# Four graph layers on 32 groups: TensorE transposes replaced by VectorE block transposes and a trip through DRAM, with layers 0 and 1 run further ahead

## Chip, cores and metric

The kernel runs on one core of a Trainium2 chip. The metric is the device time in microseconds (us) of one execution. Five engines work side by side, each through its own queue of instructions: TensorE (PE, matmuls; PEld in the profile is its loading of the stationary operand), VectorE (DVE), ScalarE (ACT), GpSimd (POOL) and SyncE (SP, which here only issues DMAs). An instruction may wait for semaphores; everything behind it in the same queue waits with it.

## What is computed

There are 128 graphs of 128 nodes with 256 features, and an integer adjacency per graph. Four layers follow each other, and each is followed by a residual sum and a LayerNorm:

```python
x = _layernorm(x + L0(x, adj, a0, a1, a2, a3))  # 4 edge scores e_k = leaky(x*a_k @ x^T), where(adj==k+1, e_k),
                                                # softmax over j, alpha @ x
x = _layernorm(x + L1(x, adj, W_msg, W_upd, bias))  # relu(x @ W_upd + mean over neighbours of x @ W_msg + bias)
x = _layernorm(x + L2(x, adj, weight, w_ih, ...))   # 3 rounds of a GRU cell:
#     m = h @ weight[i]; aggr = A^T @ m
#     r = sigmoid(i_r + h_r); z = sigmoid(i_z + h_z); n = tanh(i_n + r * h_n); h = (1 - z) * n + z * h
x = _layernorm(x + L3(x, adj, W, a))  # Wh = x @ W; e = leaky(f_i + f_j); softmax(where(adj > 0, e, -1e9)); elu(alpha @ Wh)
```

All is in 32-bit floats, and the output has the shape of x.

## The kernel before

Four graphs make a group (G = 4, T = 4 x 128 = 512 columns), so there are 32 groups (NG). A matrix of one group stands either "tokens first" (128 nodes on the partitions, graph and feature along the row) or "features first" (128 of the 256 features on the partitions, KC = 2 such halves, and 512 graph-and-node columns). A PE matmul contracts over the partitions, so the kernel turns matrices from one form into the other again and again. It does so on PE: a transpose is a matmul against the identity `ident`, which writes a PSUM bank, from which ACT or DVE copies it to SBUF.

- `head(g)` holds layers 0 and 1 of group g. It loads x and adj, turns x (`features_first`, L236/L237), does four rounds of scaled scores (POOL and ACT make `xs`, PE L308, a predicated copy L309), a softmax, turns the probabilities (`columns_first`, L261/L263), multiplies by x (L328), normalises, turns x1 (L236), then layer 1: the product with W_upd and W_msg (L349), the product with the adjacency (L358), LayerNorm, and turns x2 into hT (L236).
- `gru(s)` holds layer 2. Each of its NL = 3 rounds has, for each half c, an aggregate over neighbours (`aggregate`, L406, copied to `agT` by ACT L410) and gates: `terms` (L418) adds products with the hidden state hT (`w_hhT`) and with the aggregate (`c_gi`) in one PSUM bank. `hidden` (L426), `reset` (L431, L432), `candidate` (L436 add, L438 tanh, L440 subtraction on POOL) and `update` (L446 tanh, L447, L449) make the new state. The aggregate needs the state tokens first: `tokens_first` (L390) turns it, `h_tokens` (L395) copies it to SBUF.
- `tail(g)` holds layer 3: it turns the GRU's result (L390, added at L509), statistics, the product with w3 (L519), a broadcast by transpose (L529), the masked softmax, the turn of the probabilities (L261), the product (L556), ELU (L560 to L570), LayerNorm and the output DMA (L575).

`run` writes the order of emission: `gru(g)` is the main line, `tail(g-1)` and `head(g+1)` are side lines. Every `yield took, gap, pe` gives an estimate of the PE time just emitted and the time after which the line may go on; a counter `clock` adds these. The Tile framework's scheduler may still move instructions on an engine, since it orders them by its own model. All PSUM tiles come from one pool of eight banks (`bank()`), and each wait is a semaphore that the framework sets.

DMAs are issued by SP alone: two loads and one output per group. DMAs go round eight completion lanes, and a DMA first waits for the one before it on its lane.

Of the kernel before, what the change touches and what calls it, by code (L numbers as in the profile page):

```python
# [17 lines left out]
def kernel(  # L18
# [29 lines left out]

    nc = tc.nc
# [15 lines left out]
    psum = ctx.enter_context(tc.tile_pool(name="psum", bufs=8, space=bass.MemoryType.PSUM))  # L65

    def bank():
        return psum.tile([P, 512], F32, tag="ps", name="ps")
# [6 lines left out]
    def load(g):  # L75
        xg = inputs.tile([P, G, D], F32, tag="x_in", name="x_in")
        nc.sync.dma_start(out=xg, in_=x[g * G : (g + 1) * G].rearrange("b n d -> n b d"))
        ag = inputs.tile([P, G, N], I32, tag="adj_in", name="adj_in")
        nc.sync.dma_start(out=ag, in_=adj[g * G : (g + 1) * G].rearrange("b i j -> i b j"))
        return xg, ag  # L80

    loaded = {0: load(0)}


# [22 lines left out]

    def weights():

        nats = []  # L110
        for src in (w_ih, w_hh):
            nat = work.tile([P, NGC, D], F32, tag="hu", name="nat")
            nc.sync.dma_start(out=nat, in_=src.rearrange("(g p) d -> p g d", p=P))
            nats.append(nat)
            if src is w_ih:
                wnat = []
                for i in range(NL):
                    w = work.tile([P, KC, D], F32, tag="q", name="wnat", bufs=3)
                    nc.sync.dma_start(out=w, in_=weight[i].rearrange("(c p) e -> p c e", p=P))
                    wnat.append(w)  # L120
# [10 lines left out]
        w_ihT = [work.tile([P, 3 * D], F32, tag="wh", name="w_ihT") for c in range(KC)]  # L131
        for nat, dst in zip(nats, (w_ihT, [w_hhT[:, c] for c in range(KC)])):
            for c in range(KC):
                for g0, g1 in ((0, 4), (4, NGC)):
                    ps = bank()
                    for g in range(g0, g1):
                        nc.tensor.transpose(
                            ps[:, (g - g0) * P : (g - g0 + 1) * P], nat[:, g, c * P : (c + 1) * P], ident
                        )
                    nc.any.tensor_copy(dst[c][:, g0 * P : g1 * P], ps[:, : (g1 - g0) * P])  # L140
                    yield 0.4, 0.0


        for i in range(NL):
# [7 lines left out]
            nc.any.tensor_copy(wT, ps.rearrange("p (e d) -> p e d", e=KC))  # L152
            yield 0.4, 1.0
            for d in range(KC):
                for n0, n1 in ((0, 512), (512, 3 * D)):
# [9 lines left out]
                    nc.any.tensor_copy(c_gi[:, i, d, n0:n1], ps[:, : n1 - n0])  # L165
# [24 lines left out]

    def statistics(res, out):
# [3 lines left out]
        for b in range(G):  # L197
# [3 lines left out]
            if b == 1:  # L201
                yield 0.0, 1.5, False
        nc.vector.tensor_scalar_add(rstd, mv[:, :, 1], EPS)  # L203
        nc.gpsimd.tensor_tensor(rstd, rstd, neg_half, OP.pow)  # L204
        out.extend((mv, rstd))

    def normalise(res, mv, rstd, tag, bufs, out):
        nmr = work.tile([P, G], F32, tag="nmr", name="nmr", bufs=4)
        nc.vector.scalar_tensor_tensor(nmr, mv[:, :, 0], -1.0, rstd, op0=OP.mult, op1=OP.mult)  # L209
        xn = work.tile([P, G, D], F32, tag=tag, name=tag, bufs=bufs)  # L210
        for b in range(0, G, 2):
            nc.vector.tensor_scalar(
                xn[:, b, :], res[:, b, :], mv[:, b, 0:1], rstd[:, b : b + 1],
                op0=OP.subtract, op1=OP.mult,
            )
        yield 0.0, 0.5, False
        for b in range(1, G, 2):
            nc.scalar.activation(  # L218
                xn[:, b, :], res[:, b, :], AF.Identity, bias=nmr[:, b : b + 1], scale=rstd[:, b : b + 1]
            )  # L220
        out.append(xn)

    def layernorm(res, tag, bufs, out):
        got = []
        yield from statistics(res, got)
        yield 0.0, 2.5, False
        yield from normalise(res, *got, tag, bufs, out)

    def features_first(xn, tag, bufs):

        xT = []
        for c in range(KC):
            t = work.tile([P, T], F32, tag=tag, name=tag, bufs=bufs)
            ps = bank()
            for b in range(G):
                nc.tensor.transpose(ps[:, b * N : (b + 1) * N], xn[:, b, c * P : (c + 1) * P], ident)  # L236
            nc.scalar.copy(t, ps)  # L237
            xT.append(t)
        return xT

    def softmax(alpha, out):
# [4 lines left out]
        p = work.tile([P, G, N], F32, tag="prob", name="prob", bufs=3)  # L246
# [6 lines left out]
        yield 0.0, 3.0, False  # L253
        rinv = work.tile([P, G], F32, tag="rinv", name="rinv", bufs=4)
        nc.vector.reciprocal(rinv, rs)
        out.extend((p, rinv))

    def columns_first(p):
        ps = bank()
        for b in range(G):  # L260
            nc.tensor.transpose(ps[:, b * N : (b + 1) * N], p[:, b, :], ident)  # L261
        pT = work.tile([P, G, N], F32, tag="probT", name="probT")
        nc.scalar.copy(pT, ps.rearrange("p (b n) -> p b n", b=G))  # L263
        return pT
# [6 lines left out]

    def head(g, s):
        xg, ag = loaded.pop(g)
# [4 lines left out]
        a_f = work.tile([P, G, N], F32, tag="a_f", name="a_f")  # L282
        nc.gpsimd.tensor_copy(a_f, ag)
        alpha = work.tile([P, G, N], F32, tag="alpha", name="alpha")
        nc.gpsimd.memset(alpha, NEG0 / SLOPE)
        mk = work.tile([P, 4, G, N], U8, tag="mk", name="mk")
        s.m_gt = work.tile([P, G, N], U8, tag="m_gt", name="m_gt", bufs=3)
        s.a_ne = work.tile([P, G, N], F32, tag="a_ne", name="a_ne")


        xT = features_first(xg, "xT", 4)
        yield 0.9, 1.0, False
        for k in range(4):
            nc.vector.tensor_scalar(mk[:, k], a_f, float(k + 1), None, op0=OP.is_equal)
            yield 0.0, 1.0
            ps = bank()
            xs = []
            for c in range(KC):
# [5 lines left out]
                xs.append(t)  # L304
            for b in range(G):
# [3 lines left out]
            nc.vector.copy_predicated(alpha.rearrange(FLAT), mk[:, k].rearrange(FLAT), ps)  # L309
            yield 1.8, 0.5, False  # L310
        yield 0.0, 0.5, False

        leaky(alpha, alpha, 0.0)
        nc.vector.tensor_scalar(s.m_gt, a_f, 0.0, None, op0=OP.is_gt)
        yield 0.0, 1.5, False
        got = []
        yield from softmax(alpha, got)
        p, rinv = got
        nc.vector.tensor_scalar(s.a_ne, a_f, 0.0, None, op0=OP.not_equal)
        yield 0.0, 0.0  # L320
        pT = columns_first(p)
        yield 0.45, 1.5
        res = work.tile([P, G, D], F32, tag="res", name="res", bufs=3)
# [11 lines left out]
        yield 1.75, 2.0, False  # L335
        got = []
        yield from layernorm(res, "xa", 1, got)
        x1 = got[0]
        yield 0.0, 2.0


        xT = features_first(x1, "xT", 4)
        yield 0.9, 2.0
        hu = work.tile([P, G, 2 * D + 1], F32, tag="hu", name="hu")
        nc.gpsimd.memset(hu[:, :, 2 * D : 2 * D + 1], 1.0)
        for b in range(G):
            ps = bank()
            for c in range(KC):
                nc.tensor.matmul(  # L349
                    ps, xT[c][:, b * N : (b + 1) * N], w_um[:, c, :], start=(c == 0), stop=(c == KC - 1)  # L350
                )
# [3 lines left out]
        res = work.tile([P, G, D], F32, tag="res", name="res", bufs=3)  # L355
        for b in range(G):
# [14 lines left out]
            if b % 2:  # L371
                yield 0.9, 2.5, b == 1
        got = []
        yield from layernorm(res, "xb", 3, got)
        s.x2 = got[0]
        yield 0.0, 2.0
        s.hT = features_first(s.x2, "hT", 8)
        yield 0.9, 1.5

    def gru(s):
        hT = s.h0T = s.hT
        hn = [s.x2[:, :, c * P : (c + 1) * P] for c in range(KC)]

        def tokens_first(c, h):

# [268 lines left out]
```

## Time and profile before

| what | us |
|---|---|
| time, median of 3 runs (lowest to highest) | 3246.43 (3245.19 to 3246.86) |
| the profiled execution, its time | 3246.94 |
| span of the profiled execution on the core | 3245.2 |
| mean granted PE clock | 0.992 |
| first GRU matmul (L418) starts | 77.7 |
| GRU matmuls of one group, PE passes of 512 columns | 144 |
| last GRU matmul starts; last output DMA issued | 3210.6; 3241.4 |

A line of groups in the profile reads: line, engine, operation, tile written<-tiles read, shape, xcount | busy us, mean ns of one | idle time of the engine before them and what ended it. "Busy" of PE overlaps: matmuls are pipelined, so the time that one adds to PE's path is read from starts in the timeline, not from its mean. In this trace one 32-bit matmul stands as two PE instructions, and a transpose as one. A chain line tells which work the last instruction can be followed back through. "PEld issue" is time in which nothing that the profile shows is waited for. A line of DMA issues ends with the median us from issue to landing.

The groups of the GRU's elementwise work lie at 0.68 to 0.72 us for 128x512 on ACT and DVE, and at 1.3 us on POOL (L440). Every sixth to eighth group is 1.6 us longer than the others.

### The profile page before, as it was taken

The numbers are of one execution on the slowest core, as the hardware profiler recorded it, in microseconds if no ns is written. First come the engines' busy times: TensorE is split into PE (matmuls) and PEld (weight loads), VectorE is DVE, ScalarE is ACT, GpSimd is POOL, SyncE is SP. The second block draws the span as 40 slices with busy tenths as digits, with TensorE's granted clock in tenths as the row PEclk, the third lists the DMA queues.
The fourth block names the chain that finished last, engine by engine and source line by source line (L and its number), as shares of the span: only waits on it lengthen the run. The fifth ranks groups of instructions, "written<-read, shape, count | busy, mean of one in ns | idle before, by whom it ended". The sixth has DMA issues, their size and how long they took to land.

```text
span 3245.2 us, 32948 instructions
## 1 busy us (share of the span) xinstructions
PE 3137.9 (97%) x11992; PEld 1836.3 (57%) x11992; DVE 1563.0 (48%) x4022; ACT 1362.6 (42%) x2768; POOL 802.4 (25%) x679
## 2 busy tenths in 40 slices
PE   7999999999999999999999999999999999999997
PEld 4556555556555565555565555555555655555654
DVE  3445455544455454545444554545454445544443
ACT  3344434444344444344444444444444444444443
POOL 2122222222221222222222212222212222122221
PEclk8999999999999999999999999999999999999998
DMA  2000000000000000000000000000000000000000
GB/s 80 10 14 10 11 17 17 17 13 11 10 17 17 14 11 10 17 17 17 14 10 11 17 17 14 10 11 17 17 17 14 11 10 17 13 14 1 7 7 13
DMA packets 56995, 47.60 MB, mean 15 GB/s; under 512 B 4353, under 2 KB 56705, under 8 KB 56833
## 3 DMA queue, kind: packets, MB, share of 16 engines
q1 hardware_dynamic: 56832, 45.50, 4.4%
q8 instruction: 95, 1.56, 0.2%
q14 instruction: 68, 0.55, 0.1%
HBM read 28.72 MB, written 16.78 MB: 14 GB/s over the span
## 4 chain that ended last, share of the span: by engine, by line
PE 79%; DVE 10%; POOL 5%; ACT 4%; issue 1%; DMA 0%; ACTq 0%; POOLq 0%; SPq 0%; DVEq 0%
PE ps L418 49%; PE ps L349 7%; PE ps L308 7%; PE ps L406 4%; PE ps L519 3%; PE ps L390 3%; DVE st L199 3%; POOL rstd L204 2%; DVE res L570 2%; POOL res L566 2%; PE ps L236 2%; PE ps L358 2%; DVE res L331 2%; ACT res L563 1%; ACT xa L218 1%
## 5 line engine op out<-in xcount | busy, mean ns | idle before, releaser
L418 PE MATMUL ps<-hT,w_hhT 128*128 128x512 f32 x2304 | 1088.8, 593 | 0.0
L418 PE MATMUL ps<-agT,c_gi 128*128 128x512 f32 x2304 | 1061.6, 592 | 0.0
L418 PEld LDWEIGHTS ps<-agT,c_gi 128*128 128x128 f32 x2304 | 430.1, 190 | 466.9 <-issue 453.5
L418 PEld LDWEIGHTS ps<-hT,w_hhT 128*128 128x128 f32 x2304 | 406.3, 191 | 342.5 <-issue 319.0
L440 POOL TENSOR_TENSOR t_d<-hT,t_n 128x512 f32<-128x512 f32 x192 | 248.8, 1296 | 984.4 <-ACT t_n L438 596.1
L447 DVE SCALAR_TENSOR_TENSOR t_d<-t_z,t_d 128x512 f32<-128x512 f32 x192 | 132.3, 689 | 433.3 <-ACT t_z L446 377.8
L349 PE MATMUL ps<-w_um,xT 128*128 128x512 f32 x512 | 251.6, 616 | 63.4 <-ACT xT L237 63.4
L308 PEld LDWEIGHTS ps<-xs,xT 128*128 128x128 f32 x2048 | 249.9, 193 | 60.7 <-issue 53.8
L432 DVE SCALAR_TENSOR_TENSOR t_r<-t_r,q 128x512 f32<-128x512 f32 x192 | 134.5, 700 | 306.0 <-ACT t_r L431 306.0
L204 POOL TENSOR_TENSOR rstd<-rstd,neg_half 128x4 f32<-128x4 f32 x128 | 143.0, 1117 | 559.7 <-DVE rstd L203 559.7
L308 PE MATMUL ps<-xs,xT 128*128 128x128 f32 x2048 | 250.4, 276 | 0.0
L426 ACT ACTIVATE q<-ps,bhn 128x512 f32<-128x512 f32 x192 | 131.9, 687 | 278.0 <-PE ps L418 278.0
L301 POOL TENSOR_SCALAR xs<-xT,acol 128x512 f32<-128x512 f32 x128 | 201.0, 1576 | 136.3 <-PE ps L308 123.5
L446 ACT ACTIVATE t_z<-ps,brz 128x512 f32<-128x512 f32 x192 | 131.9, 687 | 203.8 <-PE ps L418 203.8
L199 DVE BATCH_NORM_STATS2 st<-res 128x6 f32<-128x256 f32 x512 | 200.7, 408 | 1.1
L349 PEld LDWEIGHTS ps<-w_um,xT 128*128 128x128 f32 x512 | 94.8, 195 | 184.5 <-ACT xT L237 95.9
L431 ACT ACTIVATE t_r<-ps,brz 128x512 f32<-128x512 f32 x192 | 130.4, 679 | 159.0 <-PE ps L418 159.0
L410 ACT COPY agT<-ps 128x512 f32<-128x512 f32 x192 | 112.8, 588 | 181.3 <-PE ps L406 173.5
L218 ACT ACTIVATE xb<-res,nmr,rstd 128x256 f32<-128x256 f32 x128 | 73.4, 598 | 271.8 <-DVE nmr L209 271.8
L309 DVE COPY_PREDICATED alpha<-mk,ps 128x512 f32<-128x512 uint8 x128 | 93.1, 728 | 193.2 <-PE ps L308 193.1
L438 ACT ACTIVATE t_n<-t_r,bih 128x512 f32<-128x512 f32 x192 | 138.7, 723 | 110.4 <-DVE t_r L436 110.4
L406 PEld LDWEIGHTS ps<-a_ne,hn 128*128 128x128 f32 x1024 | 134.2, 191 | 34.5 <-issue 31.1
(97 smaller groups left out, 3506.3 us busy)
## 6 DMA issues: line engine op xcount, KB each, us to landing
x_in<-in_x_dram SPq DMA_DIRECT2D x32, 512.0 KB, 3.4
out_dram<-xb SPq DMA_DIRECT2D x32, 512.0 KB, 2.9
adj_in<-in_adj_dram SPq DMA_DIRECT2D x32, 256.0 KB, 2.7
nat<-in_L_gnn_w_ih_dram SPq DMA_DIRECT2D x1, 768.0 KB, 5.1
wnat<-in_L_gnn_weight_dram SPq DMA_DIRECT2D x3, 256.0 KB, 5.5
nat<-in_L_gnn_w_hh_dram SPq DMA_DIRECT2D x1, 768.0 KB, 7.3
w_um<-in_L_gnn_W_upd_dram SPq DMA_DIRECT2D x1, 256.0 KB, 7.6
w_um<-in_L_gnn_W_msg_dram SPq DMA_DIRECT2D x1, 256.0 KB, 7.4
```

What stands on the lines that cost most here:

```text
L199: nc.vector.bn_stats(st, res[:, b, :])
L204: nc.gpsimd.tensor_tensor(rstd, rstd, neg_half, OP.pow)
L301: nc.gpsimd.tensor_scalar(t, xT[c], acol[:, k, c : c + 1], None, op0=OP.mult)
L308: nc.tensor.matmul(ps[:, cols], xT[c][:, cols], xs[c][:, cols], start=(c == 0), stop=(c == KC - 1))
L349: nc.tensor.matmul(ps, xT[c][:, b * N : (b + 1) * N], w_um[:, c, :], start=(c == 0), stop=(c == KC - 1))
L406: nc.tensor.matmul(ps[:, b * N : (b + 1) * N], hn[c][:, b, :], s.a_ne[:, b, :], start=True, stop=True)
L418: nc.tensor.matmul(gates[q], w[:, q * P : (q + 1) * P], v, start=(start and n == 0), stop=(stop and n == len(ops) - 1),)
L426: nc.scalar.activation(t, ps, AF.Identity, bias=bhn[:, c : c + 1], scale=0.5)
L432: nc.vector.scalar_tensor_tensor(t, t, 1.0, q, op0=OP.add, op1=OP.mult)
L438: nc.scalar.activation(n, t, AF.Tanh, bias=bih[:, 2 * KC + c : 2 * KC + c + 1], scale=1.0)
L440: nc.gpsimd.tensor_sub(d, hT[c], n)
L447: nc.vector.scalar_tensor_tensor(d, z, 1.0, d, op0=OP.add, op1=OP.mult)
```

## The change

The change does five things.

1. Transposes no longer go through PE and PSUM, except for the weights and the broadcast in layer 3. The new `turned` lets DVE transpose blocks of 32x32 inside a [128, 512] matrix, writes the result to a DRAM tile with four DMAs, one for each 32 partitions, in runs of 32 floats (128 bytes), and reads it back with one DMA in rows of 512 floats, so that the blocks stand where the full transpose has them. It is used for layer 0's and layer 3's probabilities, for x1 (two halves), for hT (two), and for the new state of each half in each round (six): 12 times a group.
2. x is loaded a second time as blocks: eight DMAs of 32x16x32 floats per group, and two DVE transposes make the features-first form (the old load of rows stays, for the product and the residual).
3. `head` is split into `layer0` and `layer1`; while `gru(g)` runs, the side lines are layer 3 of g-1, layer 1 of g+1 and layer 0 of g+2. Layers 0 and 1 of group 0 and layer 0 of group 1 run ahead of the first GRU.
4. The scheduler no longer reorders: `manual_schedule` keeps each engine in the order of emission. `run` now emits a piece of the GRU's matmuls, up to two side steps without PE, the GRU's elementwise step, then one side step with PE. The GRU's order within a round is new: all products with the hidden state come first, then both aggregates, then the rest.
5. PSUM has two tags of four banks each: "gate" for the r and z gates, "ps" for all else. LayerNorms normalise in place; two steps of layer 3 and the softmax exponentials are emitted in halves.

```diff
-    psum = ctx.enter_context(tc.tile_pool(name="psum", bufs=8, space=bass.MemoryType.PSUM))
+    psum = ctx.enter_context(tc.tile_pool(name="psum", bufs=4, space=bass.MemoryType.PSUM))
+    dram = ctx.enter_context(tc.tile_pool(name="dram", bufs=4, space=bass.MemoryType.DRAM))
+    ctx.enter_context(tc.manual_schedule())
+    def bank(tag="ps"):
+        return psum.tile([P, 512], F32, tag=tag, name=tag)
...
     def load(g):
+        xb = inputs.tile([P, KC, 4 * G, 32], F32, tag="x_blocks", name="x_blocks", bufs=1)
+        for c in range(KC):
+            for j in range(4):
+                f0 = c * P + j * 32
+                nc.sync.dma_start(
+                    out=xb[j * 32 : (j + 1) * 32, c],
+                    in_=x[g * G : (g + 1) * G, :, f0 : f0 + 32].rearrange("b (i r) f -> r (b i) f", r=32),
+                )
...
+    def turned(dst, src):
+        n = src.shape[1]
+        z = work.tile([P, 4, n, 32], F32, tag="z", name="z", bufs=3)
+        nc.vector.transpose(z.rearrange("p j n f -> p n j f"), src.rearrange("p n (j f) -> p n j f", f=32))
+        way = dram.tile([32, 4, n, 4, 32], F32, tag="way", name="way")
+        for i in range(4):
+            nc.sync.dma_start(
+                out=way[:, :, :, i, :].rearrange("f j n t -> f (j n) t"),
+                in_=z[i * 32 : (i + 1) * 32].rearrange("f j n t -> f (j n) t"),
+            )
+        nc.sync.dma_start(
+            out=dst, in_=way.rearrange("f j n i t -> j f (n i t)")
+        )
...
     def softmax(alpha, out):
...
-        out.extend((p, rinv))
+        pT = work.tile([P, G, N], F32, tag="probT", name="probT")
+        turned(pT, p)
+        out.extend((pT, rinv))
...
+    def layer0(g, s):
+        ag, xb = loaded.pop(g)
...
+            nc.vector.transpose(t, xb[:, c].rearrange("p i f -> p (i f)"))
...
+        yield from softmax(alpha, got)
+        pT, rinv = got
+        yield 0.0, 7.5
...
+    def layer1(g, s):
+        x1, a_f = s.x1, s.a_f
+        xT = work.tile([P, G, KC, N], F32, tag="x1T", name="x1T", bufs=1)
+        for h in range(2):
+            turned(
+                xT[:, 2 * h : 2 * h + 2].rearrange("p b c n -> p (b c n)"),
+                x1[:, 2 * h : 2 * h + 2].rearrange("p b (c n) -> p (b c) n", c=KC),
+            )
+            yield 0.0, 1.0, False
...
+        yield 0.0, 7.0
         for b in range(G):
             ps = bank()
             for c in range(KC):
-                    ps, xT[c][:, b * N : (b + 1) * N], w_um[:, c, :], start=(c == 0), stop=(c == KC - 1)
+                nc.tensor.matmul(ps, xT[:, b, c, :], w_um[:, c, :], start=(c == 0), stop=(c == KC - 1))
...
+        for c in range(KC):
+            t = work.tile([P, T], F32, tag="hT", name="hT", bufs=8)
+            turned(t, res[:, :, c * P : (c + 1) * P])
...
                 nc.vector.scalar_tensor_tensor(new[c], d, 0.5, n, op0=OP.mult, op1=OP.add)
+                tokens[c] = work.tile([P, G, P], F32, tag="hn", name="hn", bufs=4)
+                turned(tokens[c].rearrange(FLAT), new[c].rearrange("p (b n) -> p b n", b=G))
+            both = [0, 1]
+            terms(R, of_h=[0], start=True)
+            terms(R + 1, of_h=[0], start=True)
+            yield 1.7
+            yield 0.0
+            terms(Z, of_h=[0], start=True)
+            terms(Z + 1, of_h=[0], start=True)
+            yield 1.7
+            yield 0.0
+            c0 = terms(C, of_h=both, start=True, stop=True)
+            yield 1.7
+            q0 = hidden(0, c0)
+            yield 0.0
...
             aggregate(0)
+            yield 0.9
+            yield 0.0
...
+            r0 = terms(R, of_m=both, stop=True)
+            yield 1.7
+            t0 = reset(0, r0, q0)
+            yield 0.0
...
+            hT, hn = new, tokens
...
+        for n, took in enumerate(main):
+            if n % 2 == 0:
+                clock[0] += took
+                for _ in range(2):
+                    l = first(False)
+                    if l:
+                        l.go()
+            else:
+                l = first(True)
+                if l:
+                    l.go()
...
+    run((), weights(), chain(layer0(0, states[0]), layer1(0, states[0])), chain(pause(15.0), layer0(1, states[1])))
     for g in range(NG):
         side = []
         if g:
-            side.append(tail(g - 1, states[g - 1]))
+            side.append(layer3(g - 1, states[g - 1]))
         if g + 1 < NG:
-            side.append(head(g + 1, states[g + 1]))
-        run(gru(states[g]), *side)
+            side.append(layer1(g + 1, states[g + 1]))
+        if g + 2 < NG:
+            side.append(layer0(g + 2, states[g + 2]))
+        run(gru(g, states[g]), *side)
```

In the new kernel L226 is the DVE transpose of `turned`, L229 its writes and L233 its read; L335 are layer 0's scores, L351 its product with the probabilities, L384 layer 1's product with the weights, L391 that with the adjacency, L431 the aggregate, L443 the gates' matmuls, L457, L461, L463, L465, L471 to L474 the GRU's elementwise steps; L550 adds the GRU's result for layer 3, L560 is its product with w3, L594 that with the probabilities, L598, L601, L605, L606 and L610 the ELU.

## The prediction

> **What bounds the kernel now.** I read the totals first, then the chain of waits.
>
> ```profile
> PE 3137.9 (97%) x11992; PEld 1836.3 (57%) x11992; DVE 1563.0 (48%) x4022; ACT 1362.6 (42%) x2768; POOL 802.4 (25%) x679
> PE 79%; DVE 10%; POOL 5%; ACT 4%; issue 1%; DMA 0%; ACTq 0%; POOLq 0%; SPq 0%; DVEq 0%
> ```
>
> TensorE (PE) is busy almost throughout. The 21% of the chain on other engines is mostly cover: the chain runs through them while PE has other work. The PE timeline (start, us, what, idle before in brackets) shows what is wait, and the list of waits sums it (us, times, longest).
>
> ```profile
> 1608.98 3.60 PE L418 MATMUL ps<-agT,c_gi 128*128 128x512 f32 x8
> 1614.68 3.64 PE L349 MATMUL ps<-w_um,xT 128*128 128x512 f32 x4 [2.10 <-ACT xT L237]
> 1618.15 0.60 PE L390 MATMUL ps<-ident,hT 128*128 128x128 f32 x4
> 1618.59 1.88 PE L349 MATMUL ps<-w_um,xT 128*128 128x512 f32 x4
> ...
> PE ps L349 <- ACT xT L237: 63.4, 31, 2.1
> ```
>
> The starts tell the price on PE: four transposes take 1618.15 to 1618.59, 0.11 us each; four passes over 512 columns 1.72 us (1618.59 to the next start, 1620.31), so a matmul (two passes) 0.86 us. The only regular PE wait is the one in brackets, layer 1's features after layer 0's LayerNorm. Output DMAs stand 98.8 us apart, so a group is 98.8 us of which 2.1 is wait.
>
> **What the change removes.** The transposes of PE, in the groups by line and form (busy us, mean ns, idle before):
>
> ```profile
> L390 PE MATMUL ps<-ident,hT 128*128 128x128 f32 x768 | 110.7, 273 | 2.5 <-DVE hT L449 2.5
> L261 PE MATMUL ps<-ident,prob 128*128 128x128 f32 x256 | 39.3, 275 | 3.4 <-ACT prob L249 3.2
> L236 PE MATMUL ps<-ident,x_in 128*128 128x128 f32 x256 | 35.0, 282 | 4.7 <-DMA x_in<-in_x_dram 4.7
> L236 PE MATMUL ps<-ident,xb 128*128 128x128 f32 x256 | 34.2, 278 | 7.3 <-DVE xb L212 7.3
> L236 PE MATMUL ps<-ident,xa 128*128 128x128 f32 x256 | 34.1, 277 | 4.5 <-DVE xa L212 4.5
> ```
>
> These are 1792 transposes (56 a group); at 0.11 us of PE's path (not 0.275, which overlaps) that is 196 us. With layer 1 a group ahead the 63.4 us wait has nothing left to be late. 3245.2 - 196 - 63 = 2986. ACT also loses its copies of transposes out of PSUM (68.5 + 37.0 + 37.8 + 37.7 us); it wasn't the limit, so nothing.
>
> **What it adds.** Each `turned` is one VectorE (DVE) transpose of 128x512, four DMAs to DRAM and one back: 12 a group. The x load becomes eight DMAs beside two DVE transposes. Layer 0 two groups ahead and layer 1 one ahead do the same PE work at another time: no price, except where their trips meet on SP. So DVE gets 14 transposes, SP 71 DMAs a group instead of 3, the DMA engines 28,672 packets of 128 bytes. Rows that price them, of the groups by line, of the DMA issues (median us to landing at the end) and, last, of SP's timeline (start, us):
>
> ```profile
> L395 DVE COPY hn<-ps 128x512 f32<-128x512 f32 x64 | 43.9, 686 | 69.7 <-PE ps L390 69.7
> L570 DVE SCALAR_TENSOR_TENSOR res<-neg,res 128x512 f32<-128x512 f32 x64 | 73.6, 1189 | 74.5 <-POOL res L566 74.5
> L440 POOL TENSOR_TENSOR t_d<-hT,t_n 128x512 f32<-128x512 f32 x192 | 248.8, 1296 | 984.4 <-ACT t_n L438 596.1
> ...
> out_dram<-xb SPq DMA_DIRECT2D x32, 512.0 KB, 2.9
> adj_in<-in_adj_dram SPq DMA_DIRECT2D x32, 256.0 KB, 2.7
> 1.77 2.03 SPq L92 DMA_DIRECT2D acol<-in_L_gnn_a_dram  x4
> ```
>
> No DVE transpose is in the trace. Bounds: 0.42 us (the cheapest 128x512 row, L294) and 1.19 (L570, the dearest); I take 0.69, the copy it is nearest to. DVE then stands at 48.8 + 14 x 0.69 - 2 x 0.69 = 57 us a group: below PE, but it now works in the order of emission.
>
> A 128-byte packet isn't there either. The trace's packet records have 4 bytes at 9 ns, 144 at 12, 512 at 27, 1024 at 46, 2048 at 96. I take 13.5 ns, on the line between them, bounds 9 and 27. At 13.5 the small packets fill 16 engines 24 us of a group, at 27 48 us: capacity is not the limit, latency is.
>
> One write of 512 packets puts 32 on each engine: out's 2.9 us less 32 x 46 ns plus 32 x 13.5 ns is 1.86 us to landing. The four are issued 0.51 us apart (the acol row, back to back). The read moves 256 KB like adj_in: 2.6 us (its 2.7, with 8 x 96 for 32 x 27 ns). A trip after the DVE transpose: 0.1 + 1.53 + 1.86 + 0.1 + 2.6 = 6.2 us, and SP is held 4.0 of them, since the read waits for the writes and stands in front of the next trip. Low end (9 ns, issues at the steady 0.37, read 2.1 by first packet 1.03 + 0.77 + 0.33): trip 5.1, hold 3.3. High end (27 ns: the writes' own 3.46 us rule): 7.7 and 5.5.
>
> [...]
>
> **Where PE would wait.** I walked the program's own order by hand with the trace's durations (512-wide ACT 0.69, DVE 0.67, POOL subtract 1.30, pow 1.1, four exponentials 1.65, four LayerNorm statistics 1.5). Clock zero: start of the reset matmuls of a group's second GRU round. On PE the two resets end at 3.44, candidate 0 at 5.16, update 0 at 6.88, candidate 1 at 8.60, update 1 at 10.32.
> - Layer 0's probability trip starts at 2.1 and lands at 8.3; its matmuls (L351 of the new kernel) come at 10.32. No wait; 2 us of cover.
> - DVE gives new[0] at 9.4, turned at 10.1. Then layer 3's probabilities (turned 10.9) and two normalisations stand before candidate 1's add, done at 12.5. ACT has t_n at 13.3, two normalisations, then update 1's tanh at 15.1. The gate pool has four banks, so the next round's second update gate waits for that tanh: PE is there at 14.65. **0.5 us.**
> - SP takes new[0]'s trip at 10.2 and holds to 14.2; layer 3's probabilities then land at 20.3; PE reaches L594 at 19.45. **0.85 us.**
> - Before the third round's aggregate copies ACT has four Relus (behind DVE's L598), two normalisations and an exponential: the first copy ends at 27.8, PE is there at 27.2. **0.6 us.**
> - Group boundary, clock zero at the third round's resets: two L610 (1.19 each) and a new[0] transpose delay candidate 1's add to 12.4, update 1's tanh to 13.9; the next group's gate wants the bank at 12.9. **1.0 us.**
> - SP holds for new[1] from 16.7 to 20.7, issues out, then layer 1's first trip from 21.2: lands 27.3. PE comes to L384 at 25.3. **2.0 us.** Queued behind it: the second half of x1T and the x load, each with over 5 us of cover.
> - First to second round: over 3 us of cover everywhere, since L335, L560 and L391 lie between.
>
> Sum 5.0 us a group, 31 groups: 155.
>
> Ends: the prologue gets 13 more SP issues (6.6 us) before the weights and four trips in place of PSUM copies (some 12 us), less 8.9 us of layer 0 of group 1, done there in PE's idle time: +10. The last layer 3 has two trips on its path (+6.0, +5.0) and halves two steps (-2): +9.
>
> **Sum.** 2986 + 19 + 155 = 3160 us of span. The profiled run was 3246.9 with a span of 3245.2; the median is 1.2 over the span: 3161.
>
> **Rivals.**
> - *PE waits nowhere*: 3005 + 1 = 3006. For it: the waits are 0.5 to 2 us, sums of many small steps, and a delay in one place gives slack in the next. Against: every engine is now in order, and the four-bank pools were eight free banks.
> - *One SP queue too slow (slower than before)*: at 27 ns a packet layer 3's trip lands at 23.3 (3.85 us) and layer 1's at 30.3 (5.0): with 0.5 + 0.6 + 1.0 it is 11 a group, 3005 + 341 + 1 = 3347. It decides when the waits pass (3245 - 3005) / 31 = 7.75 us a group, a trip of 6.9 us. For it: nothing in the trace writes small pieces to DRAM, and the holds add up behind each other. Against: 144 bytes at 12 ns.
> - *DVE transposes at 1.19 us*: three of them stand before candidate 1's add (+1.45 on the gate bank), one in the next round (+0.5), two before x1T (+1.0), and the aggregate copy +0.4: 8.3 a group, 3263. Against: L570 is the odd one among rows of this size.
> - That transposes stay on PE can be left out: the built order has none of the 56 left (four broadcasts a group remain).
>
> **Numbers.** Forecast 0.48 (own range 3075 to 3235), no waits 0.12, SP queue 0.30, DVE 0.10. 3161 is the likeliest. The range 3050 to 3350 takes the low end's sum (2.2 us a group: 3074) and most of the rival without waits, up to the high end. About 0.2% is what a measurement tells from no change: faster 0.61, same 0.05 (waits within 0.2 us of 7.75), slower 0.34.
>
> **What would show it.** PE: no L236, L261, L390; waits on DMA at L384 and L594, on ACT at the gates of L443, none at L351. DMA issues: writes to `way` landing in 1.9 us, reads in 2.6. DVE transposes of 0.69. Wrong, if trips land past 6.9 us, if PE waits at L431 for the tokens (5 us of cover by my walk), or if a wait of DVE on a DMA (L550) holds the gates' work behind it.

## The result and the profile after

The changed kernel takes 3897.89 us (median of 4 runs, 3897.48 to 3909.01) against 3245.93 (3245.19 to 3246.86) for the kernel before beside it: a ratio of 1.2017, 95% interval 1.1995 to 1.2038. It is slower by a fifth, and the forecast of 3161 was wrong in sign; its range ended at 3350. The profiled run is one of 3897.48 us with a span of 3895.7.

The totals and the chain of waits, the two lines that the prediction began with:

```profile
PE 3153.5 (81%) x10200; PEld 1726.1 (44%) x10200; DVE 1929.2 (50%) x4411; ACT 1187.0 (30%) x2479; POOL 830.6 (21%) x711
PE 42%; DVE 21%; DMA 19%; ACT 6%; SPq 5%; issue 4%; POOL 3%; DVEq 0%; POOLq 0%; ACTq 0%
```

1792 PE instructions are gone, as forecast, yet PE is busy 16 us longer than before, and DMA stands on 19% of the chain in place of 0%. Both have to be explained. The waits of PE (total us, times, longest) say where it stands:

```profile
PE ps L384 <- DMA x1T<-way: 314.0, 31, 12.0
PE ps L594 <- DMA probT<-way: 185.0, 29, 14.8
PE ps L351 <- DMA probT<-way: 75.8, 32, 14.5
PE ps L431 <- DMA hn<-way: 51.1, 8, 13.6
PE gate L443 <- DMA hT<-way: 20.2, 1, 20.2
PE gate L443 <- ACT t_z L471: 15.7, 27, 0.8
PE gate L443 <- ACT agT L435: 14.9, 26, 0.6
```

The two places are those forecast, L384 and L594, at 314.0 / 31 = 10.1 us and 185.0 / 29 = 6.4 us in place of 2.0 and 0.85.

The stretches from the first to the last GRU matmul, first of the kernel before, then of the changed one (start:end, length, busy us and instructions of PE, PEld, DVE, ACT, POOL, granted PE clock, share of the DMA engines, GB/s):

```profile
77.70:3212.40 3134.70, 3071.53 (x11727) 1789.05 (x11726) 1519.44 (x3888) 1329.57 (x2696) 782.97 (x653) 1.00 0.04 13
```

```profile
119.60:3839.00 3719.40, 3082.65 (x9916) 1675.86 (x9916) 1861.91 (x4238) 1154.14 (x2399) 799.02 (x675) 0.91 0.33 68
```

These settle the account. PE's idle time there is 3719.4 - 3082.7 = 637 us; it was 63, and the forecast has 155. PE's busy time should have fallen by the 196 us of transposes and the 8.9 us of layer 0 that moved ahead; it rose by 11, so it is 216 us longer than forecast. Most of this is the clock, 0.91 in the mean for 1.00: the trace's clock records put 345 us of PE's busy time in the stretch at 0.50, against 14 in the kernel before, and half of the difference, 165 us, is lost. Of the other 51 us, some 28 may be PE's stops (an estimate: 206 in place of 31, each with the 0.16 us by which a row's busy time, 1.88, exceeds its step from start to start, 1.72); the rest stays open. The two ends together grew from 110.5 to 176.3 us, 65.8 for a forecast of 19 + 8.9. So 482 (waits) + 216 (longer busy time) + 38 (ends) = 736 us, which is 3895.7 less the forecast span of 3160.

How a long wait makes the matmuls behind it slow is seen on PE's timeline (start, us, what, idle before in brackets) and, next, in windows over it:

```profile
1899.14 3.78 PE L384 MATMUL ps<-w_um,x1T 128*128 128x512 f32 x4 [11.12 <-DMA x1T<-way]
1902.72 2.45 PE L443 MATMUL gate<-agT,c_gi 128*128 128x512 f32 x4
1905.01 1.88 PE L384 MATMUL ps<-w_um,x1T 128*128 128x512 f32 x4
```

```profile
1887.00:1899.00 12.00, 1.02 (x10) 0.83 (x8) 1.64 (x3) 1.21 (x2) 0.00 (x0) 0.63 0.46 101
1899.00:1903.00 4.00, 3.86 (x5) 1.79 (x6) 0.00 (x0) 0.04 (x1) 0.00 (x0) 0.50 0.15 36
1905.00:1912.00 7.00, 7.00 (x30) 4.12 (x29) 4.35 (x11) 2.36 (x4) 0.00 (x0) 1.00 0.45 86
```

After 11 us without work four passes take 3.58 us from start to start (1899.14 to 1902.72) instead of 1.72, and the next four 2.29; the granted clock is 0.50 there and 1.00 from 1905 on. This wait cost 2.4 us on top of its 11.1. By the clock records the full clock came back at 1903.86, 4.7 us after the matmuls began. Over the whole stretch all 62 waits above 4 us end at 0.50, of the 144 shorter ones three do, and after the 58 above 5 us the way back took 4.9 us in the median.

The trips themselves are read from SP's timeline. The first two lines are a trip that meets no other, the next four two trips one behind the other:

```profile
1826.25 2.57 SPq L229 DMA_DIRECT2D way<-z  x4
1830.50 0.56 SPq L233 DMA_DIRECT2D probT<-way  x1
...
1878.49 2.59 SPq L229 DMA_DIRECT2D way<-z  x4
1884.32 0.56 SPq L233 DMA_DIRECT2D hn<-way  x1
...
1885.43 5.37 SPq L229 DMA_DIRECT2D way<-z  x4
1893.65 0.56 SPq L233 DMA_DIRECT2D x1T<-way  x1
```

Alone, the writes need 4.25 us until the read is issued (forecast 3.5: they are issued some 0.64 apart, not 0.51, and 0.46 us pass between their last packet and the read, not 0.1). Behind another trip they need 5.8, and behind a trip and an output (issued at 1884.98) 8.2. And the read itself, from its issue to the end of its last 2 KB packet in the packet records, takes 5.0 us in the median, where the forecast has 2.6. Over all 384 trips the median from first write to last read packet is 11.05 us and the hold of SP 6.44, for a forecast of 6.2 and 4.0.

What makes the read slow is in the same packet records. A 2 KB packet takes 84 ns in the median; in the changed kernel 3.6 of them are under way on average while any is, and more than four in 9% of that time. In the read issued at 1830.50 the 2 KB packets run in four streams, 80 ns from start to start in each, and each stream ends in one packet of 4 bytes. All 43 reads behind which SP issues nothing for 5.6 us have four such packets, where each write of the trip from 1826.25 has 16, and so has each load of `adj_in` after the prologue in the kernel before. The DRAM side of the read is `way.rearrange("f j n i t -> j f (n i t)")`, whose outermost dimension is j, of four. So the author's reading is that four engines carry the read, one for each j; the records name no engine, and the first run below tests it. The forecast took the read to be like the load of `adj_in`, spread over 16.

### The profile page after: what moved, and what is told of

Read it like the earlier page. It is cut to its first block, busy times and chain, and to the rows that moved or that the text cites. A ratio compares the mean times of both kernels' runs of the same rounds, so it can differ in the third digit from the quotient of the medians.

```text
span 3895.7 us, 33430 instructions
## 1 busy us (share of the span) xinstructions
PE 3153.5 (81%) x10200; PEld 1726.1 (44%) x10200; DVE 1929.2 (50%) x4411; ACT 1187.0 (30%) x2479; POOL 830.6 (21%) x711
## 4 chain that ended last, share of the span: by engine, by line
PE 42%; DVE 21%; DMA 19%; ACT 6%; SPq 5%; issue 4%; POOL 3%; DVEq 0%; POOLq 0%; ACTq 0%
PE gate L443 17%; DMA way<-z 9%; PE ps L384 7%; PE ps L443 6%; PE ps L335 5%; DMA probT<-way 4%; DMA x1T<-way 4%; SPq L229 4%; POOL t_d L465 3%; PE ps L560 3%; DVE z L226 3%; DVE t_d L472 2%; PE ps L594 2%; ACT t_n L463 2%; DVE t_r L461 2%
## 5 line engine op out<-in xcount | busy, mean ns | idle before, releaser
L443 PE MATMUL gate<-hT,w_hhT 128*128 128x512 f32 x1536 | 776.8, 636 | 35.9 <-DMA hT<-way 20.2
L443 PE MATMUL gate<-agT,c_gi 128*128 128x512 f32 x1536 | 740.3, 612 | 14.9 <-ACT agT L435 14.9
L384 PE MATMUL ps<-w_um,x1T 128*128 128x512 f32 x512 | 297.3, 712 | 317.4 <-DMA x1T<-way 314.0
L443 PEld LDWEIGHTS gate<-agT,c_gi 128*128 128x128 f32 x1536 | 297.2, 199 | 369.8 <-issue 308.3
L443 PEld LDWEIGHTS gate<-hT,w_hhT 128*128 128x128 f32 x1536 | 308.3, 204 | 338.4 <-issue 254.6
L465 POOL TENSOR_TENSOR t_d<-hT,t_n 128x512 f32<-128x512 f32 x192 | 243.7, 1269 | 817.0 <-ACT t_n L463 817.0
L443 PE MATMUL ps<-agT,c_gi 128*128 128x512 f32 x768 | 361.9, 594 | 0.0
L443 PE MATMUL ps<-hT,w_hhT 128*128 128x512 f32 x768 | 351.1, 592 | 0.2 <-DVE hT L474 0.2
L463 ACT ACTIVATE t_n<-t_r,bih 128x512 f32<-128x512 f32 x192 | 138.6, 722 | 598.0 <-DVE t_r L461 594.5
L384 PEld LDWEIGHTS ps<-w_um,x1T 128*128 128x128 f32 x512 | 110.4, 223 | 453.2 <-DMA x1T<-way 320.8
L457 DVE SCALAR_TENSOR_TENSOR t_r<-t_r,q 128x512 f32<-128x512 f32 x192 | 131.4, 685 | 329.6 <-ACT t_r L456 329.5
L335 PEld LDWEIGHTS ps<-xs,xT 128*128 128x128 f32 x2048 | 251.7, 194 | 79.7 <-issue 44.4
L335 PE MATMUL ps<-xs,xT 128*128 128x128 f32 x2048 | 263.1, 280 | 24.5 <-POOL xs L326 14.1
L594 PE MATMUL ps<-wh,probT 128*128 128x256 f32 x256 | 96.6, 515 | 185.0 <-DMA probT<-way 185.0
L443 PEld LDWEIGHTS ps<-agT,c_gi 128*128 128x128 f32 x768 | 144.0, 191 | 170.0 <-issue 169.5
L443 PEld LDWEIGHTS ps<-hT,w_hhT 128*128 128x128 f32 x768 | 143.6, 190 | 155.8 <-issue 141.0
L456 ACT ACTIVATE t_r<-gate,brz 128x512 f32<-128x512 f32 x192 | 131.9, 687 | 224.3 <-PE gate L443 224.1
```

The costliest lines, as they stand in the source:

```text
L335: nc.tensor.matmul(ps[:, cols], xT[c][:, cols], xs[c][:, cols], start=(c == 0), stop=(c == KC - 1))
L384: nc.tensor.matmul(ps, xT[:, b, c, :], w_um[:, c, :], start=(c == 0), stop=(c == KC - 1))
L443: nc.tensor.matmul(gates[q], w[:, q * P : (q + 1) * P], v, start=(start and n == 0), stop=(stop and n == len(ops) - 1),)
L456: nc.scalar.activation(t, ps, AF.Tanh, bias=brz[:, c : c + 1], scale=0.5)
L457: nc.vector.scalar_tensor_tensor(t, t, 1.0, q, op0=OP.add, op1=OP.mult)
L463: nc.scalar.activation(n, t, AF.Tanh, bias=bih[:, 2 * KC + c : 2 * KC + c + 1], scale=1.0)
```

## The experiments

All 12 runs are compared with the kernel before, run beside them on the same chip. Trip is the median from the first write's issue to the end of the last read packet, hold that from the first write's issue until SP is free again (not taken where other writes stand between a trip's writes and its reads); PE idle is span less busy. Trip, hold, busy and idle are those of the profiled run, which for the read by 128 rows is its fastest, 3457.21.

| kernel | us (median) | ratio, 95% interval | trip; hold | PE busy | PE idle |
|---|---|---|---|---|---|
| changed | 3897.89 | 1.1995 to 1.2038 | 11.05; 6.44 | 3153.5 | 742 |
| read by 128 rows | 3479.49 | 1.0706 to 1.0742 | 6.63; 4.58 | 3056.4 | 399 |
| later use | 3579.10 | 1.1007 to 1.1051 | 11.21; 6.80 | 3107.7 | 466 |
| read by rows, later use | 3378.66 | 1.0395 to 1.0426 | 6.62; 4.59 | 3050.9 | 326 |
| four reads | 3602.49 | 1.1079 to 1.1116 | 7.26; 6.01 | 3115.1 | 486 |
| four reads, later use | 3246.12 | 0.9991 to 1.0010 | 7.26; 6.02 | 3007.1 | 240 |
| the same, reads set apart | 3251.22 | 1.0005 to 1.0024 | not taken | 3008.1 | 241 |
| the same, six z | 3244.21 | 0.9988 to 1.0006 | 7.27; 6.01 | 3003.1 | 240 |
| reads apart and six z | 3247.95 | 0.9996 to 1.0015 | not taken | 3016.0 | 236 |
| changed, reads set apart | 3853.54 | 1.1849 to 1.1896 | not taken | 3165.7 | 687 |
| PE transposes in the new order | 3196.55 | 0.9835 to 0.9864 | none | 3117.5 | 78 |
| sides by trip | 3272.14 | 1.0067 to 1.0097 | 7.28; 6.03 | 3079.9 | 189 |
| one kind of trip | 3210.57 | 0.9878 to 0.9911 | 7.19; 5.96 | 3094.6 | 114 |

### Is it the read on four engines?

```diff
-        nc.vector.transpose(..., src.rearrange("p n (j f) -> p n j f", f=32))
+        nc.vector.transpose(..., src.rearrange("p n (f j) -> p n j f", j=4))
...
-            out=dst, in_=way.rearrange("f j n i t -> j f (n i t)")
+            out=dst, in_=way.rearrange("f j n i t -> (f j) (n i t)")
```

> Undoes one thing: the DRAM side of the trip's read walks 128 contiguous rows instead of 4 columns of blocks; bytes, instructions, writes and order stay. Theory A (the read's 2 KB packets run on about 4 of the 16 DMA engines, 5.5 us instead of the predicted 2.6): read about 2.6 to 3 us, trip about 7 in place of 9.7, SP held some 2.7 us less for each trip, so that PE's waits at L384 (12.0 longest) and L594 (14.8) shrink to about 2 to 5 us each, L351 and L431 nearly vanish, and the granted clock comes back towards 0.97: 3200 to 3450 us. Rival B (the write phase of 4.25 us and the single queue of SP set the pace, the read's length is mostly hidden): trips get 1 us shorter at most and the time stays over 3700. Rival C (a DVE transpose with a source step of four columns is slower): DVE rows over 1 us each, and waits on DVE appear on PE.

Measured: 3479.49 us, 418 less. The read falls from 5.0 to 2.35 us, with 11.2 packets under way on average. PE's waits on DMA fall to a third (waits of PE, as above):

```profile
PE ps L384 <- DMA x1T<-way: 106.7, 31, 5.6
PE gate L443 <- ACT t_z L471: 80.1, 59, 2.0
PE ps L594 <- DMA probT<-way: 53.0, 19, 12.6
```

B falls. A holds for the read, the trip (6.63) and the clock (0.968 in the profiled run), but the time lies 29 us above its range. C is true too, and no run tells how much of the 29 us is its share. DVE's transposes now read every fourth column; the first row is the changed kernel's, the second this one's (busy, mean ns):

```profile
L226 DVE STREAM_TRANSPOSE z<-hT 128x512 f32<-128x512 f32 x192 | 136.6, 711 | 6.5
```

```profile
L226 DVE STREAM_TRANSPOSE z<-hT 128x512 f32<-128x512 f32 x192 | 211.7, 1103 | 6.5
```

Four reads, one for each 32 partitions, spread the packets too (7.1 under way, 2.94 us from the first issue to the last packet) and leave DVE's source without the step. The rows that one read walks lie as far apart in DRAM as before, so the read is faster than 5.0 us without that change of order too:

```diff
-        nc.sync.dma_start(
-            out=dst, in_=way.rearrange("f j n i t -> j f (n i t)")
-        )
+        for j in range(4):
+            nc.sync.dma_start(
+                out=dst[j * 32 : (j + 1) * 32], in_=way[:, j].rearrange("f n i t -> f (n i t)")
+            )
```

> Like the first experiment (the read on 16 engines), but by four reads of 32 rows of 2 KB, so that the DVE transpose keeps its contiguous source (0.69 instead of 1.1 us). Theory A: the read phase falls from 5.5 to about 2.5 to 3 us (three more issues of 0.35, 2 packets per engine and read), trip about 7.2; with DVE as short as in the changed kernel, less than the first experiment's 3479: 3250 to 3400 us, L384 and L594 the rest. If instead DVE's 0.4 us for each of 12 transposes meant nothing, 3430 to 3500, as in the first experiment. If the three more issues make SP the limit: over 3500.

Measured: 3602.49 us, so the third branch, although DVE is back at 0.7 us. The trip is 7.26 and SP is held 6.01 us instead of 4.58. L385 and L595 are the changed kernel's L384 and L594:

```profile
PE ps L385 <- DMA x1T<-way: 174.4, 31, 8.5
PE ps L595 <- DMA probT<-way: 146.3, 27, 13.1
```

What counts for both places is the hold of the trip in front plus the trip itself, and the forecast's own walk gives the price. PE comes to L384 8.1 us after SP takes the trip in front (25.3 - 16.7, less 0.5 for out), to L594 9.25 us after (19.45 - 10.2).

| | hold + trip | L384: by the walk; measured | L594: by the walk; measured |
|---|---|---|---|
| forecast | 10.2 | 2.1; - | 0.95; - |
| read by 128 rows | 11.2 | 3.1; 3.4 | 2.0; 2.8 |
| four reads | 13.3 | 5.2; 5.6 | 4.0; 5.4 |
| changed kernel | 17.5 | 9.4; 10.1 | 8.2; 6.4 |

At L384 the walk, given the measured pair, comes within 0.7 us at all three kernels. At L594 it misses by 0.8 to 1.8 us, to both sides. So the walk was right in kind; its two numbers were not.

### Is it lateness, or the capacity of SP's queue?

The distances between a trip and its matmuls are pauses in the order of emission (layers 0, 1 and 3):

```diff
-        yield 0.0, 7.5    # layer 0
+        yield 0.0, 11.0
-        yield 0.0, 7.0    # layer 1
+        yield 0.0, 19.0
-        yield 0.0, 5.5    # layer 3
+        yield 0.0, 14.0
```

> Only the three distances between a trip and its matmuls are enlarged in the order of emission (layer 0 from 7.5 to 11, layer 1 from 7 to 19, layer 3 from 5.5 to 14 us); the trips stay as slow as they are. If the trips are merely late (the queue has the capacity): PE finds its operands there, waits at L384, L594 and L351 fall under 50 us each, clock back to about 0.98: 3050 to 3250 us. If SP's queue is short of capacity (12 trips of 6 to 8 us held each group, about 85 of 99 us, and they bunch): the waits only move, to L431 (tokens) or to the gates, and the time stays over 3500.

Measured: 3579.10 us, the second case in time. The regular waits on trips at L384 and L594 are gone (one of 14.8 us is left at L594), and other waits have come, at L431 as that case has it and at L335 in place of the gates:

```profile
PE ps L431 <- DMA hn<-way: 152.9, 34, 5.8
PE ps L335 <- POOL xs L326: 144.8, 29, 13.8
```

The tokens' trips have no pause to lengthen. Why L335 waits is seen on the chain of waits (start, us, what):

```profile
1836.92 2.49 DVE xd L258 x2
1839.41 0.62 DVE z L226
1840.03 0.60 DVE xT L312
...
1840.72 1.58 POOL xs L326
...
1842.35 1.78 PE ps L335 x5
```

The transposes of x's blocks (L312), which layer 0 of the next group starts from, stand on DVE behind layer 3's LayerNorm (L258), and that ends late. Part of it is that L258 takes 1.22 us a step there in the mean, where the same step takes 0.41 in the other LayerNorms and, in the run with PE transposes below, at this place too; why is not shown. Distance alone does not make slow trips free: what comes later stands in front of other work on an engine that keeps the order.

The two edits together, once with the read by 128 rows and once with four reads, both with smaller pauses:

```diff
-        yield 0.0, 7.5    # layer 0
+        yield 0.0, 9.0
-        yield 0.0, 7.0    # layer 1
+        yield 0.0, 12.0
-        yield 0.0, 5.5    # layer 3
+        yield 0.0, 9.0
```

> The first edit (read by rows) with moderately larger distances (9, 12 and 9 us). If the length of the read is the cause and the rest is lateness, PE waits hardly any more: about 3005 us and the sum of leftovers, 3030 to 3150 us, below the kernel before. If the queue of SP or the write phase is the limit, over 3400.

> Four reads and distances of 9, 12 and 9 us. The run with rows and these distances (3379) had the chain on DVE, whose 12 strided transposes of 1.1 us each stood before the gates. Theory A: with 0.69 us, PE waits on ACT and DVE fall to some 2 us a group and none is left on DMA: 3050 to 3200 us. Rival: what the bunch of DVE work at the third round costs does not come from the transposes' length, then 3330 to 3400.

Measured: 3378.66 and 3246.12 us. In the first, PE no longer waits regularly on trips but for ACT's `agT` (120.3 us in 29 waits), and the chain runs through DVE, where transposes of 1.1 us stand among the gates' work. With four reads and 0.7 us the time is 132 us lower, although the trip is longer (7.26 for 6.62), which is as the theory had it in kind, but the theory's range ended at 3200. This kernel is level with the kernel before: all that the lost transposes gave is spent on what is left. Its waits, with L432 the tokens of L431:

```profile
PE ps L432 <- DMA hn<-way: 65.2, 25, 12.9
PE gate L444 <- DVE hT L475: 25.2, 29, 0.9
```

Two ideas on that rest were tried. In one the reads go into SP's order 3 us of that order's own clock later, so that SP does not stand and wait for the writes. In the first of the two runs this puts the reads of 97 of the 384 trips behind the next trip's writes, in the second those of 152:

```diff
+        def read():
...
+        later.append((clock[0] + 3.0, read))
```

> The version with four reads and longer distances (3246), but each trip's reads are put into SP's order 3 us of the order's own clock later, behind the writes of the next trip, so that SP does not stand waiting (667 us of SP waiting for the writes there, 6.0 us held a trip). Theory (SP's hold, not the trip's length, is what is left): SP's wait on the writes falls below 250 us, PE's wait for tokens at L431 (65 us) nearly goes, 3100 to 3200 us. Rival (the rest is DVE's bunch in front of the gates): 3220 to 3260, no change.

> The changed kernel with nothing else than the reads put later in SP's order in the same way; the read stays on 4 engines, 5 us, distances as they are. If the hold of SP (6.4 us a trip, 74 of 119 us a group) makes the trips late: 3550 to 3750 us. If the trip's own length (4.3 + 5.0 us against 7 us of distance at most) makes them late: 3800 to 3950, no gain.

Measured: 3251.22 and 3853.54 us. SP's wait on the writes fell from 667 to 304 us in the first and from 997 to 381 in the second, and the time changed by +5 and -44. More than half of SP's standing is gone in the first without a gain (the theory had asked for less than 250), so that standing by itself is not what costs there. A read that SP issues behind eight writes lands no earlier: layer 1's two trips in (`x1T`) take 8.92 us in the median, 7.70 before. As a test of hold against length the second run is weak for the same reason: `x1T` takes 12.63 us instead of 11.95 and its wait stays (318 us for 314), while that of layer 3's probabilities falls from 185 to 141.

In the other, DVE gets six buffers `z` instead of three, since the chain showed 2.1 us of a DMA before two of its transposes around the change from the second GRU round to the third:

```diff
-        z = work.tile([P, 4, n, 32], F32, tag="z", name="z", bufs=3)
+        z = work.tile([P, 4, n, 32], F32, tag="z", name="z", bufs=6)
```

> The version with four reads and longer distances (3246), with six buffers in place of three for the transposed blocks z that the writes read from. There, DVE stood 2.1 us twice a group before a transpose, waiting for the writes of an earlier trip to give its z back, and the gates' work stood behind it. Theory (the write phase reaches PE through DVE): those waits go, 4 us a group less on the path at the third round: 3110 to 3190 us. Rival (the third round's DVE work is too long by itself): 3230 to 3250.

> The same six buffers in the version whose reads stand later in SP's order (3251). With z free, SP's order is all that is between writes and reads: 3090 to 3190 us if SP's hold still costs anything once DVE is free of the writes, so less than the run with six buffers alone; equal to it if it does not.

Measured: 3244.21 and 3247.95 us, no change. The chain's step was not DVE's limit. Windows over the run with six buffers point to what is (the second round's gates, then the start of the third, in which PE waits):

```profile
1818.00:1832.00 14.00, 13.51 (x44) 7.06 (x42) 13.30 (x40) 7.14 (x20) 2.33 (x2) 1.00 0.32 56
1832.00:1848.00 16.00, 14.02 (x44) 7.80 (x44) 11.95 (x31) 5.50 (x11) 4.00 (x4) 1.00 0.44 85
```

DVE (the third busy time) is full for 13.3 of 14 us, so the new state is late, its trip starts late behind the one before it, and the tokens come 1.7 us after PE. What share of the remaining 240 us of idleness DVE's bunch and the trip have each stays open.

### Is it the new order, with engines that keep to it?

Each trip is replaced by PE transposes and a copy out of PSUM where the result is used; order, pools and layers ahead stay, and the pauses in front of the matmuls shrink to 1 to 1.5 us:

```diff
-        turned(pT, p)
+        nc.scalar.copy(pT, on_pe(lambda b: p[:, b, :]).rearrange("p (b n) -> p b n", b=G))
```

> Keeps the changed kernel's order of emission, in-order engines, pool sizes and layers ahead, and the x blocks on DVE, but every trip through DRAM is replaced by TensorE transposes and a copy out of PSUM at the place of use. If the trips alone cost the time: 3005 + 48 transposes x 32 groups x 0.11 us = 3174, with some waits for the copies 3180 to 3280, so about the time of before. Rival D (the hand-written order and the in-order engines cost the time): over 3400 with waits of PE on ACT and DVE.

Measured: 3196.55 us, ratio 0.9849 (0.9835 to 0.9864): 1.5% faster than the kernel before and the best of all. Without the trips, the order and the in-order engines cost nothing that shows. PE waits almost nowhere; the largest regular entry, after a single one in the prologue, is

```profile
PE ps L624 <- ACT probT L301: 11.2, 30, 1.5
```

With 1536 transposes at 0.11 us taken off, it also gives the floor that the forecast worked with: 3195.2 - 169 = 3026 us of span, 21 over the forecast's 3005.

Then, would some trips pay? First the six of the side layers, with four reads and long distances; then only layer 1's output, which has a round of slack. The second edit against the version with PE transposes (the first has the same for the probabilities and for x1, with pauses of 9, 12 and 9):

```diff
-            nc.scalar.copy(t, on_pe(lambda b: res[:, b, c * P : (c + 1) * P]))
+            turned(t, res[:, :, c * P : (c + 1) * P])
```

> The version with TensorE transposes at the place of use (3197), but the six trips a group of the side layers (layer 0's and layer 3's probabilities, layer 1's two halves in and two blocks out) go by DVE blocks and four reads, with distances of 9, 12 and 9 us; the GRU tokens stay on TensorE. Removes 24 of its 48 transposes a group, 24 x 32 x 0.11 = 84 us: 3115 us if no trip is late, 3115 to 3200; as SP has half the trips, none should be. Over 3200: trips cost more than the transposes they save even with room on the queue.

> The version with TensorE transposes (3197) with one kind of trip put back: layer 1's output for the GRU (two trips a group, four reads each), which nothing needs before the next group's first round. Removes 8 transposes a group and two copies on ACT: 8 x 32 x 0.11 = 28 us. If a trip pays where it has slack: 3165 to 3175 us, no wait of PE on a DMA but in the prologue. If the two transposes on DVE (0.7 us each) or the loads queued behind them on SP cost more: 3190 to 3220.

Measured: 3272.14 and 3210.57 us, both slower than without trips (3196.55). In neither does PE wait regularly for a trip. In the first it waits for DVE's new state (70.4 us) and for layer 0's scaled inputs (46.7, 30 times), behind the same LayerNorm and transposes on DVE as above; in the second a token copy on DVE, which stands behind the two transposes and their neighbours, comes 1.0 us late once a group, where the eight transposes gave 0.9:

```profile
PE ps L442 <- DVE hn L492: 29.3, 29, 1.0
```

So the price of a trip is not only its length. It also takes 0.7 us of an in-order DVE that the gates need; that this 0.7 us makes the copy late is read from DVE's order, not tested by a run of its own.

## Why the prediction was wrong

**The step that failed** is the term "The read moves 256 KB like adj_in: 2.6 us". It measured 5.0, as its packets ran in four streams (3.6 under way on average) where the forecast had 16, and it is in both of the numbers that the walk uses: the trip (6.2, measured 11.05) and, as the next trip's writes queue behind its packets, the hold (4.0, measured 6.44; with the read by 128 rows the time from the first write to the read's issue falls from 5.88 to 4.26 us in the median). A smaller part is the write phase, 4.25 us alone instead of 3.5. With the measured pair the walk gives 9.4 + 8.2 at L384 and L594 and 2.1 + 11.05 - 10.32 = 2.8 at L351; with its 2.1 us for the banks and copies that is 22.5 us a group, or 698 for 31 groups. PE's idle time between the first and last GRU matmul is 637.

**A term that was absent** is the clock: 165 us of the 216 by which PE's busy time exceeds the forecast. The forecast priced a wait at its length.

**The ends** were 38 us too cheap: the first GRU matmul starts at 119.6 instead of 77.7, after a wait of 20.2 us for hT.

**Right were** the removed transposes (1792 of them; taking 256 out in the last two runs lowers PE's busy time by 22.9 us, 0.09 each for a forecast of 0.11) and the rest of the floor (within 21 us by the run with PE transposes, where the price of a transpose stands on both sides), the packet of 128 bytes (13.5 ns, measured mean 13.6 for the writes), the DVE transpose (0.69 us, measured 0.68 to 0.71), the gate and copy waits (0.5 to 1.0 us, measured 15.7 / 27 = 0.6 and 14.9 / 26 = 0.6), and the places, but for L351, whose 2 us of cover rested on the short trip (75.8 us in 32 waits). Of the signs that the prediction named against itself, trips past 6.9 us and waits at L431 (8 times) are there; DVE also waits for trips at L550 (36.3 us in 8), but that this held the gates' work is not shown.

**The rival "One SP queue too slow"** came true in its place and beyond its point of decision (a trip of 6.9 us), but not by its cause: the packets cost what the likeliest case took. Its high end of the trip, 7.7 us, did not reach the 11.05, since the bounds were set on the price of a packet and not on how many packets of a read run at once. The rival of DVE at 1.19 us, priced at 3263, describes the run by 128 rows: a trip near the forecast's, transposes of 1.1 us, and 3479 us. There PE's busy time is 3056 - (3117.5 - 169) = 108 us above the floor's, of which the clock records give 69 to the clock (159 us busy at 0.50, 21 in the run with PE transposes).

**Even with a trip near 7 us** the change would not have brought 85 us. At 7.26 us and the distances that it has, it measures 3602; with longer distances it is level with the kernel before. Its hold and trip together are still 3.1 us over the forecast's, since the write phase is 0.8 us longer in both and the three more issues hold SP 1.3 us more. No run gave the trips a second issuing queue.

## What to carry to other kernels

Look at the outermost dimension of a DMA before its bytes: the same 256 KB took 5.0 us with four outside on the DRAM side and 3.6 packets under way on average, and 2.35 with 128 and 11.2. Where trips share an issuing queue, what a consumer sees is the hold of the trip in front plus its own trip (at L384 that came within 0.7 us in three kernels), so take both from a measured trip and not from a lone load. And price a wait of TensorE of more than some 4 us above its length: in the changed kernel all 62 such waits ended at a clock of 0.50, and the low clock cost 165 us on top of 637.

## What the runs showed that was not expected

- Writes of 128 bytes to DRAM show no surcharge in their packet records (13.6 ns on average over 786,432 packets, for 13.1 over the 131,072 of the loads of x in blocks, which have the same size). What such a write costs beyond its packet is not seen here.
- Issuing took longer behind earlier traffic: four writes that take 2.57 us of SP alone take 5.37 behind a trip and an output (1885.43 above).
- A DVE transpose of 128x512 with a source step of four columns takes 1.10 us in place of 0.71.
